# Two-layer conditional experts on one core: where the routing groups, one activation and the last layer-0 pair's products stand in the order of work

## The chip, the cores and the metric

The kernel runs on one core of a Trainium2 chip. A core has five engines that run side by side, each with its own queue of instructions: TensorE (matmul), VectorE, ScalarE, GpSimd (called POOL in the profile) and SyncE (SP), which issues most DMA transfers. The metric is the device time of one execution in microseconds (us), less is better.

## The reference

Each of 16 samples has 256 positions of width 256, all in 32 bits. Layer 0 gives each sample one of 8 experts; layer 1 gives it a weighted sum of two experts and adds a shared expert.

```python
# layer 0: one expert for each sample
expert = jnp.argmax(opcode_onehot, axis=-1)
up   = einsum('bsd,bhd->bsh', x, W_up[expert])   + b_up[expert]      # 512 wide
gate = einsum('bsd,bhd->bsh', x, W_gate[expert]) + b_gate[expert]
x = x + einsum('bsh,bdh->bsd', silu(up) * gate, W_down[expert]) + b_down[expert]
# layer 1: two of 8 experts and the shared one, 1024 wide
rw = softmax(cond)
w, sel = top_k(rw, 2)
w = w / w.sum(-1)
w = w / 12 + (1 - 1 / 12) * stop_gradient(w)
mlp = lambda g, u, d: (gelu_tanh(x @ g) * (x @ u)) @ d
x = x + sum_k w_k * mlp(skill_gate[sel_k], skill_up[sel_k], skill_down[sel_k]) \
      + mlp(shared_gate, shared_up, shared_down)
```

## The kernel before

**Routing.** The samples are sorted on VectorE by their expert, so that two samples with the same expert can be worked on as a pair; the shared expert's pairs need no routing. For layer 1 the sort is recorded as a list of groups of VectorE instructions (`steps`, filled through `Recorder` and `step`). `route` (L1013) issues the next group; all its instructions have line 1017 in the profile. Most groups are one operation over 128x1024 numbers. `routes` (L1007) says how many groups are issued at the start of a quarter.

**A pair of samples.** A pair is computed with a 2x2 block scheme of seven products instead of eight (`STEPS`): A blocks are weights (`q`, and their sums `s`, made on POOL by `sums_a`, L524 to L527), B blocks are activations (and their sums, made on VectorE by `sums_b`, L517 to L519). The up projections are cut along the hidden dimension: 2 quarters in layer 0 and 4 in layer 1, each with seven steps up0 to up6 (L586) of two matmuls, or four records. Quarters are counted by `line.at`: 0 and 1 are the first single sample of layer 0, 2 and 3 the second, 4 to 11 the four layer-0 pairs (two quarters each), and 12 to 15 the first pair of samples in the shared expert, which is layer 1. For the data of this run a further layer-0 pair follows as 16 and 17, then the shared expert's next pair.

**Banks and readers.** Products accumulate in PSUM banks X, Y and Q, two of each; A and B, one each, serve the down products together with Y. up0, up1, up3 and up5 open a bank; up2 and up4 go on with the X of up0, and up6 with the Q of up3. ScalarE copies X out after up0, up2 and up4 (`copy`, L567). VectorE combines the copies with Y or Q into the four blocks of `c` (`combine`, L571): C11 after up1, C22 after up4, C21 after up5, C12 after up6. A bank can be opened again, or gone on with, once its readers are through. Then comes the activation (`act`: silu with a bias on ScalarE in layer 0, L616; gelu in layer 1, L622), the product of the two halves (L628, VectorE) and `act_sums` of it. The seven down steps (L660) are read by `early` (L677 on VectorE, or L682 on ScalarE) and `late` (L693 and L689 on VectorE).

**The order.** Everything is issued in an order that a small planner, `Line`, gives. It has a clock: each of up0 to up5 issues, adds 2, and then issues all that has come due. So a quarter is 12 long. `later(n, f)` makes f due n after now; of two things due together, the one put down first comes first. For quarter j, which begins at T and ends at T+12, up6 is due 4 after its end, the second half of a layer-0 activation 3, the activation and product 6, and the sums of the product 12. With `crowded` set, the product comes 9 after the end, behind C22 of the next quarter, and a layer-0 pair's sums of down weights 14 instead of 12 after the start of its second quarter. A pair's down steps follow its last quarter at `first`, `first + step` and so on. At the start of a quarter, `ahead` prepares later ones: the weights five quarters on, the `q` sums three on, and the sums of the next pair's x (`sums_x`) 5 after the quarter's start. The engines' queues are in order, so this order is also the order in which a waiting instruction holds up those behind it. Between quarters 11 and 12 the program branches on the number of further layer-0 pairs (`tc.Switch`).

Of the kernel before, what the change touches and what calls it, by code (L numbers as in the profile page):

```python
# [55 lines left out]
UP, SINGLE_UP = 2, 8  # L56
# [3 lines left out]
def kernel(  # L60
# [71 lines left out]
    def when_free(tag, f):  # L132

        if turns[tag] and not turns["later", tag]:
            f()
        else:
            turns["later", tag].append(f)
# [361 lines left out]

    class Pair(Unit):  # L500
        width, last = 2, False
        crowded = False
        first, step = 18, None

# [218 lines left out]
        def run(self, line, among):  # L723

            self.start()
            for j in range(self.kp):
                line.quarter(self, j)
                for k in range(6):
                    line.main(UP, lambda j=j, k=k: self.up(j, k))

                line.later(2 * UP, lambda j=j: self.up(j, 6))
                if not self.layer:
                    line.later(UP + 1, lambda j=j: self.act0(j, 1))
                if self.last and j == self.kp - 1:

                    line.later(1, lambda: self.act_half(j, 0))
                    line.later(2 * UP, lambda: self.act_half(j, 1))
                else:
                    self.ended[j] = line.clock
                    line.later(3 * UP, lambda j=j: when_free("bt", lambda: self.act(j)))  # L740
                line.later(6 * UP, lambda j=j: self.act_sums(j))
                for f in among[j] if j < len(among) else ():
                    f()
            step = self.step or (6 if self.layer else 3)
            for k in range(7):
                line.later(self.first + step * k, lambda k=k: self.down(k))
# [113 lines left out]
    l0_pairs = [Pair(next(names), 0, 2 * i) for i in range(NP1)]  # L860
# [3 lines left out]
    shared = [Pair(next(names), 1, None, (2 * i, 2 * i + 1)) for i in range(NPR)]  # L864
    pairs = [Pair(next(names), 1, 2 * i) for i in range(NP2)]
    more_pairs = [Pair(next(names), 1, 2 * NP2 + 2 * i) for i in range(MOST[1])]
    ones = [Single(next(names), 1, 2 * NP2 + i) for i in range(NS2)]
    for u in l0_pairs[:-1]:
        u.crowded = True
        u.first = 16.5  # L870
    shared[-1].last = True
    shared[-2].step = 7
# [42 lines left out]
    class Line:  # L915
# [64 lines left out]
        def quarter(self, unit, j):  # L980

            self.at += 1
            assert quarters[self.at] == (unit, j)
            self.ahead(self.at)
            self.send()
            for layer in range(2):
                for i, (*at, engines) in enumerate(announces[layer]):
                    if [unit, j] == at:
                        self.announce(layer, engines, i == 0)
            for _ in range(self.routes(unit, j)):  # L990
                self.route()

        def announce(self, layer, engines, first):

# [11 lines left out]

        def routes(self, unit, j):  # L1007

            if not unit.layer:
                return {2: 5, 3: 1}.get(self.at, 0)  # L1010
            return int(j < 3) + (unit is shared[0] and j == 0)

        def route(self):  # L1013

# [12 lines left out]
    line = Line()  # L1027
# [54 lines left out]
    def follow(units, behind=True):  # L1082
# [3 lines left out]
        if known == start + Q_AHEAD - 1:  # L1086
            u, j = quarters[known]
            u.load_q(j, behind=behind)

    run(units[0])  # L1090
    for k in arms(0):

# [10 lines left out]
        for a, p in zip(places[4:], pieces):  # L1103
            a.append(p)
        follow([*mid, *units[1], *tails[1]], behind=False)
        run([*mid, *units[1]])
        while line.routed < len(steps):
            line.route()
        for k in arms(1):
            left = ones[2 * k :]  # L1110
            rest = [*tails[1], *left[:-1], *more_pairs[:k], *shared[1 - NB :]]
            turns["xs"], turns["d"] = [0, 1], [*turns["d"], 2]
            for u in rest:
                among[u] = [[] for _ in range(u.kp)]
            if left:

                host = rest[len(left)]
                for j in range(host.kp):
                    among[host][j].append(partial(left[-1].piece, line, j, among=True))
                left[-1].po_bank, left[0].po_bank = "A", "B"  # L1120
                shared[-NB].first = 24
            follow(rest)
            run(rest)
            line.flush(1 << 30)
            line.send()
# [58 lines left out]
```

## Time and profile before

| What | Value |
| --- | --- |
| Time, median of 3 runs | 1047.77 us (1046.82 to 1048.23) |
| Profiled execution, whole time | 1047.03 us |
| Profiled execution, span | 1045.4 us |
| Granted TensorE clock, mean | 0.998 |
| TensorE, VectorE, ScalarE, POOL busy | 1035.3, 755.1, 371.0, 444.0 us |
| Matmuls | 4746 |
| HBM traffic | 150 GB/s over the span |

The span runs from the first to the last instruction of one profiled execution; the whole time has a little around it. A busy share is an average over the whole span. The views that answer for one place are the waits (who waited for whom, and how long), the timeline of one engine (start, duration, and in brackets the idle time before an instruction and what ended it), and the table by windows (busy time of each engine and the granted clock in a stretch). In the tables, `Y<-xt,q` means that tile Y was written from tiles xt and q.

### The profile page before, as it was taken

The page shows a single profiled execution, that of the slowest core. Times are in us where ns is not written, and L with a number is a line of the kernel's source. Part 1 is how long each engine was busy: PE and PEld are TensorE (multiplying, and loading weights), DVE is VectorE, ACT ScalarE, POOL GpSimd, SP SyncE. Part 2 cuts the span into 40 slices and gives each one's busy share as a digit, 9 for nine tenths or more (in the row PEclk, how much of TensorE's full clock was granted, in tenths as well). Part 3 has the DMA queues.
Part 4 walks back from the last instruction along what each step waited for, and adds up shares of the span by engine and source line. Part 5 has one row for each costly group of instructions (what it writes and reads, how often), then busy time and mean ns, then how long its engine had stood idle before and what let it go on. Part 6 is the DMA issues. An engine that isn't in the chain of part 4 may idle for free.

```text
span 1045.4 us, 14150 instructions
## 1 busy us (share of the span) xinstructions
PE 1035.3 (99%) x4746; PEld 900.7 (86%) x4746; DVE 755.1 (72%) x1213; ACT 371.0 (35%) x584; POOL 444.0 (42%) x509
## 2 busy tenths in 40 slices
PE   9999999999999999999999999999999999999998
PEld 7887888888888888888888888888888888888887
DVE  8799978878687767777777777777765235777764
ACT  2444353535333333333333333333333123333331
POOL 3865231221034665566467556755201255620000
PEclk9999999999999999999999999999999999999999
DMA  7654756657664355245425533542655445366532
GB/s 266 220 182 146 249 171 197 206 164 239 202 229 125 89 141 142 98 104 141 108 82 134 141 104 98 141 133 72 179 164 170 131 136 156 91 181 181 185 78 45
DMA packets 61118, 157.47 MB, mean 151 GB/s; under 512 B 7522, under 2 KB 27362, under 8 KB 56802
## 3 DMA queue, kind: packets, MB, share of 16 engines
q1 hardware_dynamic: 47762, 140.90, 39.8%
q0 software_dynamic: 12976, 15.21, 10.1%
q8 instruction: 42, 0.69, 0.3%
q14 instruction: 50, 0.41, 0.1%
q10 hardware_dynamic: 288, 0.26, 0.1%
HBM read 132.23 MB, written 24.12 MB: 150 GB/s over the span
## 4 chain that ended last, share of the span: by engine, by line
PE 94%; DVE 4%; issue 1%; ACT 0%; DMA 0%; SPq 0%; DVEq 0%; ACTq 0%
PE X L586 25%; PE Q L586 17%; PE Y L586 17%; PE A L660 13%; PE B L660 9%; PE Y L660 9%; PE X L758 2%; PE Q L758 1%; PE A L788 1%; DVE c L571 1%; PE B L788 1%; DVE bt L628 1%; PE Y L788 0%; DMA lg<-cond_dram 0%; DVE bt L517 0%
## 5 line engine op out<-in xcount | busy, mean ns | idle before, releaser
L567 ACT ACTIVATE cp<-X 128x512 f32<-128x512 f32 x318 | 189.5, 596 | 508.3 <-PE X L586 507.9
L628 DVE TENSOR_TENSOR bt<-c 128x1024 f32<-128x1024 f32 x105 | 144.8, 1379 | 121.9 <-ACT c L622 114.4
L586 PE MATMUL Y<-xt,q 128*128 128x256 f32 x736 | 189.5, 380 | 2.0 <-DVE c L571 1.7
L586 PE MATMUL Q<-xt,s 128*128 128x256 f32 x736 | 189.5, 380 | 0.4 <-DVE c L571 0.4
L586 PE MATMUL X<-xt,s 128*128 128x256 f32 x736 | 189.5, 380 | 0.0
L571 DVE TENSOR_TENSOR c<-cp,Q 128x512 f32<-128x512 f32 x212 | 144.4, 681 | 41.8 <-ACT cp L567 37.2
L571 DVE TENSOR_TENSOR c<-cp,Y 128x512 f32<-128x512 f32 x212 | 144.2, 680 | 22.9 <-PE Y L586 22.1
L586 PEld LDWEIGHTS Y<-xt,q 128*128 128x128 f32 x736 | 139.8, 190 | 22.4 <-DVE c L571 2.3
L586 PEld LDWEIGHTS Q<-xt,s 128*128 128x128 f32 x736 | 139.3, 190 | 21.0 <-DVE c L571 2.3
L586 PEld LDWEIGHTS X<-xt,s 128*128 128x128 f32 x736 | 139.3, 190 | 20.5 <-ACT cp L567 1.4
L487 POOL DMA_DIRECT2D out_dram<-ys x46 | 49.1, 1075 | 207.4 <-DVE ys L689 128.6
L524 POOL TENSOR_TENSOR s<-q 128x256 f32<-128x256 f32 x78 | 66.3, 849 | 150.0 <-PE Q L586 86.9
L527 POOL TENSOR_TENSOR s<-s,q 128x256 f32<-128x256 f32 x78 | 63.4, 813 | 128.8 <-PE Q L586 128.8
L660 PE MATMUL B<-bt,ds 128*128 128x256 f32 x420 | 101.3, 381 | 0.7 <-DVE ys L693 0.7
L660 PE MATMUL A<-bt,ds 128*128 128x256 f32 x420 | 100.5, 379 | 0.0
L622 ACT ACTIVATE c<-c 128x1024 f32<-128x1024 f32 x91 | 95.6, 1051 | 6.5 <-DVE c L571 6.3
L586 PE MATMUL X<-xt,q 128*128 128x256 f32 x368 | 95.3, 382 | 0.0
L660 PEld LDWEIGHTS B<-bt,ds 128*128 128x128 f32 x420 | 79.9, 191 | 12.2 <-issue 1.0
L660 PE MATMUL Y<-bt,d 128*128 128x256 f32 x376 | 90.0, 379 | 0.0
L660 PEld LDWEIGHTS A<-bt,ds 128*128 128x128 f32 x420 | 79.7, 190 | 11.2 <-issue 0.3
L517 DVE TENSOR_TENSOR bt<-bt 128x512 f32<-128x512 f32 x112 | 86.8, 775 | 0.1
L525 POOL TENSOR_TENSOR s<-s,q 128x256 f32<-128x256 f32 x78 | 78.1, 1002 | 6.1
(179 smaller groups left out, 1141.1 us busy)
## 6 DMA issues: line engine op xcount, KB each, us to landing
q<-wq_dram SPq DMA_DIRECT2D x114, 512.0 KB, 3.7
d<-wd_dram SPq DMA_DIRECT2D x22, 1024.0 KB, 6.4
s<-qsums SPq DMA_DIRECT2D x28, 512.0 KB, 4.9
xt<-x1d SPq DMA_DIRECT2D x46, 256.0 KB, 3.9
out_dram<-ys POOLq DMA_DIRECT2D x46, 256.0 KB, 4.5
ds<-dsums SPq DMA_DIRECT2D x7, 1024.0 KB, 6.2
d<-wd_dram SPq DMA_DIRECT2D x7, 513.0 KB, 5.6
bt<-x_dram SPq DMA_DIRECT2D x14, 256.0 KB, 4.7
```

The lines of the kernel that those rows point to most:

```text
L487: store = nc.gpsimd.dma_start(row(out), ys[:, :, t, :], accum_op=ALU.add)
L517: tt(t[:, 4:6, :], t[:, 0:3:2, :], t[:, 2:4, :], ALU.subtract)
L524: tt(s("S1"), a("A21"), a("A22"), ALU.add)
L525: tt(s("S2"), s("S1"), a("A11"), ALU.subtract)
L527: tt(s("nS4"), s("S2"), a("A12"), ALU.subtract)
L567: nc.scalar.activation(t, self.banks["X", j], AF.Copy)
L571: nc.vector.tensor_tensor(self.c[j][:, block].rearrange("p m s -> p (m s)"), self.copies[n, j], self.banks[tag, j], op,)
L586: nc.tensor.matmul(self.banks[tag, j][:, bass.ts(m, S)], lhsT=self.q[j][:, m, A_AT[a], :] if a in A_AT else self.s[j][:, m, S_AT[a], :], r ...
L622: nc.scalar.activation(u, u, AF.Gelu_apprx_tanh)
L628: nc.vector.tensor_tensor(t[:, 0:4, :], u, v, ALU.mult)
L660: nc.tensor.matmul(d, lhsT=src[:, j, :], rhs=self.acts[j][:, B_AT[b], :], start=OPENS[k] and j == 0, stop=j == self.kp - 1, skip_group_che ...
L758: nc.tensor.matmul(dst[:, bass.ts(half, S)], lhsT=self.q[j][:, m, 2 * half + c, :], rhs=self.xt[:, c, :], start=(c == 0), stop=(c == KD - 1),)
```

## The change

Three things in the order of work are changed; no instruction's operands are.

- Routing groups: in a pair's quarter a group is issued 5 after the start, behind what was due then (a `sums_x` put down before it), up6 of the quarter before and up2, and no longer at the start. The two groups of quarter 12 are issued in quarters 5 and 6, one each. Quarters 13 and 14, and the later ones, keep one group each.
- The activation of the first layer-0 pair's second quarter (number 5) is due 9 after its end and no longer 6, so behind the copy and C22 after up4 of quarter 6.
- The last layer-0 pair (quarters 10 and 11) is `crowded` like the others: its products come 9 after the quarter's end, and its sums of down weights 14 instead of 12 after the start of quarter 11. Its `first` stays at 18.

```diff
     class Pair(Unit):
         width, last = 2, False
+        behind = None
         crowded = False
...
                     self.ended[j] = line.clock
-                    line.later(3 * UP, lambda j=j: when_free("bt", lambda: self.act(j)))
+                    act = lambda j=j: when_free("bt", lambda: self.act(j))
+                    line.later(9 if j == self.behind else 3 * UP, act)
                 line.later(6 * UP, lambda j=j: self.act_sums(j))
...
+    for u in l0_pairs:
+        u.crowded = True
+
+    l0_pairs[0].behind = 1
     for u in l0_pairs[:-1]:
-        u.crowded = True
         u.first = 16.5
...
             for _ in range(self.routes(unit, j)):
-                self.route()
+
+                self.later(5 if unit.width == 2 else 0, self.route)
+            self.flush(self.clock)
...
         def routes(self, unit, j):
             if not unit.layer:
-                return {2: 5, 3: 1}.get(self.at, 0)
-            return int(j < 3) + (unit is shared[0] and j == 0)
+                return {2: 5, 3: 1, 5: 1, 6: 1}.get(self.at, 0)
+            return int(j < 3 and (unit is not shared[0] or j > 0))
```

## The prediction

> **What bounds the kernel.** The page first: which engine is full.
>
> ```profile
> PE 1035.3 (99%) x4746; PEld 900.7 (86%) x4746; DVE 755.1 (72%) x1213; ACT 371.0 (35%) x584; POOL 444.0 (42%) x509
> ```
>
> TensorE has no share left to win but its own gaps. In its timeline an undisturbed step (four records of 128x256) follows the one before after 0.8635 us, so 4,740 such matmuls want 1,023.2 us; from the first (6.00) to the end of the last (1,040.86) the trace has 1,034.9. About 11.7 us are lost in all: that is the ceiling of any re-ordering. Next, TensorE's waits, to see where:
>
> ```profile
> PE Y L586 <- DVE c L571: 1.7, 1, 1.7
> PE B L660 <- DVE ys L693: 0.7, 1, 0.7
> PE Q L586 <- issue: 0.5, 1, 0.5
> ```
>
> The first two are neighbours. TensorE's timeline there (start, us, engine, line, tiles; the idle before a group and its releaser in brackets):
>
> ```profile
> 91.81 1.03 PE L586 MATMUL X<-xt,q 128*128 128x256 f32 x4
> 92.68 1.03 PE L660 MATMUL B<-bt,ds 128*128 128x256 f32 x4
> 93.93 1.13 PE L586 MATMUL Y<-xt,q 128*128 128x256 f32 x4 [0.23 <-DVE ys L693]
> ...
> 101.94 1.13 PE L586 MATMUL Y<-xt,q 128*128 128x256 f32 x4 [1.70 <-DVE c L571]
> 103.75 1.73 PE L660 MATMUL B<-bt,ds 128*128 128x256 f32 x4 [0.68 <-DVE ys L693]
> 105.28 1.91 PE L586 MATMUL X<-xt,q 128*128 128x256 f32 x4
> 106.99 1.28 PE L586 MATMUL Y<-xt,q 128*128 128x256 f32 x4
> ...
> 108.96 1.03 PE L586 MATMUL X<-xt,s 128*128 128x256 f32 x4
> ```
>
> This is quarter 12, the shared expert's first, and the start of 13. From 91.81 to 108.96 there are 14 steps, worth 12.09 us; they took 17.15, so 5.06 us are lost in one place. The steps at 103.75 to 106.99 are twice as long as they should be though nothing holds them. The answer by windows says why (the third number from the end is the granted clock):
>
> ```profile
> 104.00:108.00 4.00, 4.00 (x12) 3.17 (x12) 3.97 (x7) 0.93 (x2) 0.00 (x0) 0.57 0.86 301
> ```
>
> What held TensorE is in VectorE's timeline:
>
> ```profile
> 91.80 1.74 DVE L628 TENSOR_TENSOR bt<-c 128x1024 f32<-128x1024 f32 x1
> 93.47 0.41 DVE L693 TENSOR_TENSOR ys<-dz,Y 128x256 f32<-128x256 f32 x1
> ...
> 98.15 0.61 DVE L1017 TENSOR_TENSOR wts<-wts,den 128x16 f32<-128x16 f32 x2
> ...
> 99.54 1.75 DVE L1017 TENSOR_TENSOR ys<-num 128x1024 f32<-128x1024 f32 x1
> 101.21 0.68 DVE L571 TENSOR_TENSOR c<-cp,Y 128x512 f32<-128x512 f32 x1
> ```
>
> The product at 91.80 (L628, quarter 10) stands ahead of the L693 that frees bank Y: the 0.23. Two routing groups (L1017) fill 98.15 to 101.21, 3.06 us, ahead of the combine C11 of quarter 12, which frees the Y bank that step up5 opens: the 1.70. The late L693 for B stands three instructions behind: the 0.68.
>
> The "issue" wait is in quarter 7's start, in VectorE's and ScalarE's timelines:
>
> ```profile
> 44.73 0.67 DVE L571 TENSOR_TENSOR c<-cp,Q 128x512 f32<-128x512 f32 x1
> 47.29 0.69 DVE L571 TENSOR_TENSOR c<-cp,Q 128x512 f32<-128x512 f32 x1 [1.88 <-ACT cp L567]
> ```
> ```profile
> 45.44 1.33 ACT L616 ACTIVATE c<-c,bq 128x512 f32<-128x512 f32 x2 [1.72 <-DVE c L571]
> 46.68 1.06 ACT L567 ACTIVATE cp<-X 128x512 f32<-128x512 f32 x2
> ```
>
> up6 of quarter 6 accumulates into bank Q after C22 has read it (47.29 to 47.98). C22 waited for the copy of X, and that stood behind the activation of quarter 5, which itself waited for VectorE. Between 46.53 and 49.02, two steps took 2.49 us: 0.76 lost.
>
> **The change, part by part.**
>
> *Two groups leave quarter 12.* 3.06 us of VectorE ahead of C11 go. With part 3, and every VectorE time in this stretch taken at its slow value (1.74 for the product, 0.94/0.83/0.83 for the sums: the rows beside a busy POOL), the order after is: sums of quarter 12's x end 91.88; L693 91.80 to 92.21 (TensorE wants that Y at 93.54: no wait); C22 of 11 to 92.8; product of 10 to 94.4; C21 95.0; early L677 95.4; sums of 10 to 98.05; C11 of 12 to 98.7. TensorE at its pitch wants that bank for up5 at 99.59: 0.9 to spare. C12, two L677, then L693 for B, done 100.4; the B step is due at 100.45, so 0 to 0.2 lost. Both idles go, hence the clock loss behind them.
>
> Here one rule is weighed. The trace: idles of 1.70 and 0.68 us, then a granted mean of 0.57 over 104 to 108, where the three steps from 103.75 to 108.10 took 4.35 us instead of 2.59. The span's mean of 0.998 leaves room for about 2 us so lost: this place and no other. The Trainium skill, "TensorE: Matmul & The Clock Gate", section "Why this matters for your kernels", says the clock drops when TensorE idles more than about 3 us between bursts. By it these idles were too short, the halving is no part of this stall and could stay: only 5.06 less 1.76, or 3.3, would come back. By the trace, where the halving follows the only large idle and comes nowhere else, all 5.06. I take the trace, and 0.1 off for B: **4.95**.
>
> *Where they go.* The group of four small ones (98.15 to 99.54: 1.39 us) goes into quarter 5 behind C12 of quarter 4 (ends 36.5), where VectorE then idles 2.81 us until 39.34: nothing. If that cover were gone it would cost up to 1.4. The 128x1024 comparison goes into quarter 6 behind the 44.73 row, into the 1.88 idle. It costs 1.22 (its sister z<-ats at 108.41) to 1.75 (beside POOL), so it ends 46.55 to 47.1.
>
> *Activation behind a copy.* ScalarE's copy for C22 no longer waits for 45.44: X is done 44.97, so copy 45.0 to 45.6, activation to 46.9 (its product, issued behind C22 before and after, is not late). C22 now starts when the comparison ends, 46.6 to 47.1, instead of 47.29; up6 is due 47.39 and needs C22's end plus 0.1. Saved: 0.15 to 0.76 of the 0.76; I take **0.4**. VectorE is not idle from 47.29 to 64.21, so the 0.49 us TensorE loses between 55.92 and 60.73 moves with it and stays.
>
> *Last layer-0 pair.* The product of 10 goes behind L693 and C22 (counted). That of 11 goes behind C22 of 12: its activation waits for C12 (99.3), runs 1.33, the copy follows at 100.6 to 101.2, C22 to 101.9 (up6 due 103.04), product to 103.1. It is needed first by the down product A at 104.77: 1.7 to spare, 0. POOL's down sums of this pair (84.94 to 88.5) fall behind the next quarter's q sums and its qsums store: those can run before 87, so down sums to 91.2, or 98 if the q sums stay at 89.88. First use was at 114.14, 109 now: at least 11 us of cover. No SP transfer changes its place in SP's queue.
>
> *Later groups, each from a quarter's start to behind C12.* Behind C12 VectorE mostly waits for ScalarE's gelu (the page: 121.9 us before L628, 114.4 of it for L622), about 1.1 us, what a group takes: nothing, and C11 and C12 come earlier. Where no such idle is, a price: the long group at 172.27 to 174.91 now pushes the next product to 178.3 and the L693 that frees Y to 180.5, which is when TensorE wants it: 0 to 0.3, I take 0.1. At 303 TensorE loses 0.69 behind a chain in which two routing bits (0.18) precede C11: they leave it, **0.15** back. The 0.32 lost at 115.66 hangs on C12, the table load and gelu: stays, 0 to 0.6.
>
> Sum: 4.95 + 0.4 + 0.15 - 0.1 = **5.4 us**. The profiled execution (1,045.4 span, 1,047.03 in all) becomes 1,041.6; it lies 0.74 under the median, within the runs' 1.4, so between the two bases, 1,041.6 and 1,042.4: **1,042.0**.
>
> **The rivals.**
> 1. *The clock stays lost* (10%): a remaining idle, B's or another, still costs one such window. Gain 5.4 less 1.7: 1,043.7; with a half of the idle left, 1,044.5. For it: the rule above. Against: the record.
> 2. *The stall moves to the last pair's down products* (5%, no change): product of 11 now waits for activation, copy and C22 in a row. It costs nothing until it ends after 104.77; 3 us beyond that, with a new 1.7 us clock loss, give back 4.7: about 1,047. Against it: 1.7 us of slack with slow values.
> 3. *VectorE has no room early* (5%, slower): if the stretch from 44.73 to 98 is one backlog, work put in at quarters 5 and 6 comes out at quarter 12 all the same; the 5.06 stay, and 1.75 more at up6 of quarter 6 with a clock loss of 1.7 gives 1,051. It decides if the idle before 47.29 is not really freed by the copy. For it: layer 0's stretch 50 to 92 has VectorE busy 40.38 of 42. Against: it waits for ScalarE's copies at 64.21 (0.26) and 82.34 (0.78), so no backlog lives that long.
>
> **How the numbers follow.** My forecast has 80%. Its least: 5.06 less 0.2 for B and 0.3 for the later groups, with 0.15 at quarter 7: 4.7, from the median 1,043.1; its most, with all of 0.76, 0.49, 0.69 and 0.32 back, 7.3: 1,040.1 midway between the bases. The range takes rival 1 in: 1,040.4 to 1,044.6. 0.2% (2.1 us) is what a measurement can tell from no change; forecast and rival 1 pass it: 0.90 faster; rival 2 mostly same, 0.04; rival 3 and the rest slower, 0.06.
>
> **What would show it.** PEclk full from 92 to 110; TensorE's 14 steps there in about 12.2 us; no L1017 between 90 and 100; L1017 in VectorE's idles near 36 and 45; the copy ahead of L616 near 45; L693 ahead of the 1.74 product. Wrong if the wait on c L571 stands elsewhere, above all before A near 105, or if up6 near 47 waits longer than now.

## The result, and the profile after

The changed kernel takes 1,041.32 us (median of 6 runs, 1,040.21 to 1,044.96) against 1,048.0 for the kernel before (6 runs): ratio 0.9943, 95% interval 0.9925 to 0.9962, or 6.7 us less. A second series of the same kernel gave 1,041.48 (5 runs, 1,041.14 to 1,041.77), ratio 0.9942 (0.9929 to 0.9956). The profiled execution of the first series took 1,044.96, with a span of 1,043.2; it is one of two of the eleven runs that stand at 1,044 or above. The forecast was 1,042.0. "First profile" and "second profile" below are the profiled executions of these two series (1,044.96 and 1,041.48).

Line numbers are shifted in the changed kernel: L572 is the combine, L629 the product, L678 `early`, L694 `late`, L1025 a routing group. First TensorE's timeline in quarter 12 and what follows (start, us, engine, line, tiles):

```profile
91.82 1.03 PE L587 MATMUL X<-xt,q 128*128 128x256 f32 x4
...
99.59 1.03 PE L587 MATMUL Y<-xt,q 128*128 128x256 f32 x4
100.45 1.03 PE L661 MATMUL B<-bt,ds 128*128 128x256 f32 x4
...
103.91 1.03 PE L587 MATMUL X<-xt,s 128*128 128x256 f32 x4
...
108.22 1.03 PE L587 MATMUL Y<-xt,q 128*128 128x256 f32 x4
110.63 1.10 PE L661 MATMUL A<-bt,ds 128*128 128x256 f32 x4 [1.38 <-DVE dz L678]
111.57 1.03 PE L587 MATMUL X<-xt,q 128*128 128x256 f32 x4
113.28 1.13 PE L587 MATMUL Y<-xt,q 128*128 128x256 f32 x4 [0.68 <-DVE ys L694]
```

The fourteen steps from 91.82 to 103.91 take 12.09 us, which is exactly their undisturbed time: all 5.06 us are back, and the windows of 4 us from 92 to 112 all have a granted clock of 1.00. But two idles are new, at 109 and 112. VectorE's timeline shows both sides of it:

```profile
97.72 0.69 DVE L572 TENSOR_TENSOR c<-cp,Y 128x512 f32<-128x512 f32 x1 [0.16 <-issue]
...
99.71 0.41 DVE L694 TENSOR_TENSOR ys<-dz,B 128x256 f32<-128x256 f32 x1
...
104.27 0.96 DVE L519 TENSOR_TENSOR bt<-bt 128x256 f32<-128x256 f32 x1
105.26 1.38 DVE L520 TENSOR_TENSOR bt<-bt 128x256 f32<-128x256 f32 x1
...
107.76 2.33 DVE L1025 TENSOR_TENSOR z<-ats 128x1024 f32<-128x1024 f32 x1
110.01 0.47 DVE L678 SCALAR_TENSOR_TENSOR dz<-A,d,bt 128x256 f32<-128x256 f32 x1
```

C11 of quarter 12 ends at 98.4 and the B reader at 100.1, 1.2 and 0.3 us before TensorE wants them. Two things then delay VectorE. Two sums ahead of quarter 13's C11 take 0.96 and 1.38 us, and quarter 13's routing group behind C12 takes 2.33; L678 behind the group frees bank A 1.4 us late. In the second profile of the same kernel the same four instructions are 2.2 us shorter in sum:

```profile
103.48 0.42 DVE L519 TENSOR_TENSOR bt<-bt 128x256 f32<-128x256 f32 x1
103.94 0.83 DVE L520 TENSOR_TENSOR bt<-bt 128x256 f32<-128x256 f32 x1
...
105.89 1.21 DVE L1025 TENSOR_TENSOR z<-ats 128x1024 f32<-128x1024 f32 x1
107.02 0.47 DVE L678 SCALAR_TENSOR_TENSOR dz<-A,d,bt 128x256 f32<-128x256 f32 x1
```

L678 is through at 107.5, and TensorE takes the step on A at 108.56, so there is 1.1 us to spare. TensorE's waits have neither idle:

```profile
PE Y L160 <- DVE cp L157: 1.6, 1, 1.6
PE Q L587 <- DVE c L572: 0.4, 1, 0.4
PE A L661 <- DVE dz L678: 0.4, 1, 0.4
```

That is the usual run; the 1.6 is at the start, the 0.4 on Q at 298 and the 0.4 on A at 59. ScalarE's timeline of the first profile shows the order that the second part of the change makes, the copy ahead of the activation:

```profile
45.76 0.60 ACT L568 ACTIVATE cp<-X 128x512 f32<-128x512 f32 x1 [1.34 <-PE X L587]
46.25 1.32 ACT L617 ACTIVATE c<-c,bq 128x512 f32<-128x512 f32 x2
```

In that profile the order gained nothing yet: TensorE had lost 0.6 us at up4 of quarter 6 (44.56), the group in quarter 6 ended at 47.39, and C22 and up6 came when they had come before the change (up6 at 48.09 against 48.08). In the second profile the group ends earlier, and C22 and up6 follow 0.7 and 0.6 us earlier:

```profile
45.39 1.24 DVE L1025 TENSOR_TENSOR ys<-num 128x1024 f32<-128x1024 f32 x1
46.55 0.67 DVE L572 TENSOR_TENSOR c<-cp,Q 128x512 f32<-128x512 f32 x1
```
```profile
47.45 1.03 PE L587 MATMUL Q<-bt,s 128*128 128x256 f32 x4
```

One thing about the kernel before is seen only in the list of its runs. One stretch of half clock during the work costs 1.7 of the 1,045 us and so takes the mean granted clock of an execution to 0.998 or less; all profiled executions without such a stretch have 0.999 or 1.000. Of the 70 further runs of the kernel before that were made beside the experiments, 23 have 0.998 or less (median 1,048.16) and 47 have 0.999 or more (median 1,047.56). By this count the profile that the forecast was reckoned from, with its half clock, shows the rarer case, and the usual run is only 0.6 us faster than such a run, not 1.7. What it loses instead is not known: none was profiled.

### The profile page after: what moved, and what is told of

Same layout as the page of the kernel before. It is cut to its first block, busy times and chain, and to the rows that moved or that the text cites. A ratio compares the mean times of both kernels' runs of the same rounds, so it can differ in the third digit from the quotient of the medians.

```text
span 1043.2 us, 14149 instructions
## 1 busy us (share of the span) xinstructions
PE 1033.6 (99%) x4746; PEld 900.5 (86%) x4746; DVE 760.9 (73%) x1213; ACT 371.0 (36%) x584; POOL 444.9 (43%) x509
## 4 chain that ended last, share of the span: by engine, by line
PE 88%; DVE 1%; issue 0%; ACT 0%
PE X L587 23%; PE Q L587 16%; PE Y L587 16%; PE A L661 12%; PE B L661 8%; PE Y L661 8%; PE Q L760 1%; PE X L760 1%; PE B L790 1%; PE A L790 1%; DVE bt L629 0%; DVE c L572 0%; ACT c L623 0%; DVE xt L520 0%; DVE ys L694 0%
## 5 line engine op out<-in xcount | busy, mean ns | idle before, releaser
L629 DVE TENSOR_TENSOR bt<-c 128x1024 f32<-128x1024 f32 x105 | 146.4, 1394 | 114.9 <-ACT c L623 111.8
L572 DVE TENSOR_TENSOR c<-cp,Q 128x512 f32<-128x512 f32 x212 | 144.3, 681 | 40.8 <-ACT cp L568 33.3
L572 DVE TENSOR_TENSOR c<-cp,Y 128x512 f32<-128x512 f32 x212 | 144.1, 680 | 27.1 <-PE Y L587 25.9
```

The lines of the kernel that those rows point to most:

```text
L572: nc.vector.tensor_tensor(self.c[j][:, block].rearrange("p m s -> p (m s)"), self.copies[n, j], self.banks[tag, j], op,)
L629: nc.vector.tensor_tensor(t[:, 0:4, :], u, v, ALU.mult)
```

## The experiments

Ratios are to the kernel before, run on the same chip with each set (its medians 1,047.4 to 1,048.0), with 95% intervals. The last four rows are the set whose kernel before has 1,047.4, half a microsecond less than the others, so a difference between medians of different sets is good to about half a microsecond.

| Kernel | Median us (runs) | Ratio |
| --- | --- | --- |
| changed, first series | 1,041.32 (6) | 0.9943 [0.9925, 0.9962] |
| changed, second series | 1,041.48 (5) | 0.9942 [0.9929, 0.9956] |
| no group in 13, one more in 16 | 1,041.57 (5) | 0.9948 [0.9935, 0.9962] |
| all groups at the start | 1,045.27 (15) | 0.9977 [0.9969, 0.9985] |
| routing part alone | 1,042.32 (5) | 0.9952 [0.9938, 0.9965] |
| group of 13 twice | 1,043.94 (5) | 0.9965 [0.9951, 0.9978] |
| without the activation part | 1,042.37 (5) | 0.9952 [0.9938, 0.9966] |
| last-pair part alone | 1,046.26 (21) | 0.9988 [0.9982, 0.9995] |
| activation part alone | 1,046.79 (21) | 0.9992 [0.9985, 0.9999] |
| group of 13 at the start | 1,043.93 (6) | 0.9967 [0.9955, 0.9979] |
| groups of 5, 6 at the start | 1,042.85 (5) | 0.9961 [0.9948, 0.9975] |
| both in 5 | 1,041.24 (5) | 0.9943 [0.9930, 0.9957] |
| both in 5, none in 13, one in 16 | 1,041.66 (5) | 0.9945 [0.9932, 0.9959] |

**The changed kernel again.**

> The changed kernel once more, for a second profile: the first profiled execution took 1044.96 us while four of its six runs took 1040.2 to 1041.4. Theory A (the new idles of 1.38 and 0.68 us near 109 to 113, behind quarter 13's routing group that took 2.33 us beside POOL's down sums, are not in every execution): a profile of a run near 1041 shows the group in about 1.2 us and less idle there. Theory B (the spread is elsewhere: start of the clock, the tail): the same idles of about 2 us stand near 109 to 113 and the runs differ by the time at which the full clock begins. Median 1041 to 1042.5 by both.

Theory A: the run is 3.5 us faster than the profiled one of the first series, and between 104 and 120 us TensorE loses 0.1 us instead of 2.6. The second profile's full clock began at 6.8 us instead of 7.6, which accounts for about 0.4 of the rest. The theory named the group alone; the rows above show the two sums ahead of it as the other half of the delay.

**Is it the group of quarter 13?** Issued twice:

```diff
-                for f in steps[self.routed]:
+                for f in steps[self.routed] * (2 if self.at == 13 else 1):
                     f()
```

> The changed kernel with quarter 13's one routing operation issued twice in a row (about 1.2 us more of VectorE at that place, in every execution; the result of the operation is the same). Theory A (the slower profile of 1044.96 us is that group taking 2.33 us instead of 1.21, with the L678 for A behind it): idles of about 1.4 us before A and 0.7 us before Y come back in the profile and the time is 2 to 3.5 us above the changed kernel's: 1043.5 to 1045. Rival (the group has about a microsecond to spare there, and the slow profile had another cause): within 0.7 us of 1041.4.

1,043.94, as forecast, and its waits are nearly those of the first profile; below them the two copies of the group on VectorE:

```profile
PE A L661 <- DVE dz L678: 1.5, 2, 1.3
PE Y L587 <- DVE ys L694: 0.7, 1, 0.7
```
```profile
106.04 3.43 DVE L1025 TENSOR_TENSOR z<-ats 128x1024 f32<-128x1024 f32 x2
```

The two copies take 3.43 us, 2.2 more than the 1.21 of one in the second profile (not 1.2, as was meant). So 2.2 us more of VectorE at that one place, as much as the first profile has, costs 2.5 us and makes these two idles, and the rival is out. It does not show that one slow group is enough: with 1.1 us to spare, a group of 2.3 just fits, and in the profile of the routing part alone (below; a group is L1022 there) it does:

```profile
104.97 2.23 DVE L1022 TENSOR_TENSOR z<-ats 128x1024 f32<-128x1024 f32 x1
```

TensorE does not wait behind that one. Taking the group away from quarter 13:

```diff
-                return {2: 5, 3: 1, 5: 1, 6: 1}.get(self.at, 0)
-            return int(j < 3 and (unit is not shared[0] or j > 0))
+                return {2: 5, 3: 1, 5: 1, 6: 1, 16: 1}.get(self.at, 0)
+            return int(j < 3 and (unit is not shared[0] or j > 1)) + (self.at == 16)
```

> The changed kernel, with quarter 13's routing group left out there and issued in quarter 16 instead. Theory A (that group, slowed by POOL's sums, holds the L678 and the product behind it): the idles near 109 to 113 (2.25 us more lost than before the change) go, no new one at quarter 16 where VectorE waits about 1.1 us for gelu; 2 us less than the changed kernel: 1039 to 1040. Rival (the backlog there comes from the last pair's later products, and the next instruction in line waits as long): idles of 1 us or more stay at the same place, 1041.

The groups are issued in a fixed order, so this moves quarter 13's group into quarter 14 (at 114.05) and quarter 14's into 16. 1,041.57: no gain over the usual run, which has no idle there to win, and none of its five runs is above 1,043; five runs are too few to tell whether the two slow ones of eleven are gone. My 1,039 to 1,040 was reckoned from the first profile, and missed.

**Where the routing groups stand within a quarter.** All of them back at the quarter's start, with the new counts:

```diff
-                self.later(5 if unit.width == 2 else 0, self.route)
+                self.later(0, self.route)
```

> The changed kernel, but groups of pairs are issued at the quarter's start again (the counts by quarter are the new ones: one in 5, one in 6, none in 12). My reading: nearly all the gain is in where the two groups go, not in their place within a quarter: quarter 5 and 6 at the start stand ahead of C11, so C22 of 5 and 6 come later by what VectorE does not idle, at most 1 us lost near 48; near 108 the group stands ahead of C11 and C12, the gelu comes 1.2 to 2.3 us later and the idle there is as long or longer. Expected 1041 to 1043. Rival (placing them behind C12 is what brings the time): 1044 or more.

1,045.27: the rival. More than half of the gain is lost again, 3.8 us. Its profile has one large wait, 1.96 us for the L694 that frees Y in quarter 14. So the group of quarter 13 was put back alone, and then the two early ones alone:

```diff
-                self.later(5 if unit.width == 2 else 0, self.route)
+                self.later(5 if unit.width == 2 and self.at != 13 else 0, self.route)
```

> The changed kernel with quarter 13's group alone back at the quarter's start; all others stay behind C12. Theory (the 3.9 us between the changed kernel and the one with all groups at the start come from this one group, because it delays C12, hence the gelu, the product and the L694 for Y that quarter 14 waits for): an idle of about 2 us before that Y and a half clock behind it, 1044.5 to 1046. Rival (the loss is spread over the later quarters): less than 1 us above the changed kernel.

```diff
-                self.later(5 if unit.width == 2 else 0, self.route)
+                self.later(5 if unit.width == 2 and self.at not in (5, 6) else 0, self.route)
```

> The changed kernel with the groups of quarters 5 and 6 at the quarter's start; all others stay behind C12. Theory as for the quarter 13 group: little is lost here. In quarter 5 VectorE idles afterwards; in quarter 6 C11 and C12 come 1.2 us later and C22 as before, the activation of quarter 5 (which waits for C12) 1.2 us later: 0 to 0.7 us above the changed kernel, 1041.4 to 1042.1. Rival: 1044 or more.

Quarter 13 alone costs 2.5 us (1,043.93, a little under the 1,044.5 to 1,046 I gave; its profiled execution, 1,045.12, lay within). VectorE's timeline in that execution:

```profile
104.53 2.29 DVE L1025 TENSOR_TENSOR z<-ats 128x1024 f32<-128x1024 f32 x1
106.74 0.67 DVE L572 TENSOR_TENSOR c<-cp,Y 128x512 f32<-128x512 f32 x1
107.33 0.68 DVE L572 TENSOR_TENSOR c<-cp,Q 128x512 f32<-128x512 f32 x1
107.93 0.47 DVE L678 SCALAR_TENSOR_TENSOR dz<-A,d,bt 128x256 f32<-128x256 f32 x1
109.13 2.36 DVE L629 TENSOR_TENSOR bt<-c 128x1024 f32<-128x1024 f32 x1 [0.73 <-ACT c L623]
111.41 0.68 DVE L572 TENSOR_TENSOR c<-cp,Q 128x512 f32<-128x512 f32 x1
112.01 0.41 DVE L694 TENSOR_TENSOR ys<-dz,Y 128x256 f32<-128x256 f32 x1
```

Ahead of C11 the group delays C12 (107.33), on which gelu waits, then product, C22 and the L694 for Y, and TensorE waits 1.96 us. Behind that the clock is halved (two windows; the first figures are length and TensorE's busy time, the third from the end is the granted clock):

```profile
109.33:112.75 3.42, 1.46 (x7) 0.98 (x6) 3.42 (x4) 0.85 (x2) 1.64 (x2) 1.00 0.75 274
112.75:116.16 3.41, 3.41 (x9) 2.71 (x9) 2.71 (x6) 0.00 (x0) 0.00 (x0) 0.50 0.47 192
```

That is the slowest of its six runs; two of the six lost the clock by their mean (0.998 or less), as did 4 of the 15 with all groups at the start and none of the changed kernel's eleven. Behind C12 the group lies where VectorE would wait for gelu anyway: in the run with no group in 13 the product waits 1.13 us for it. The groups of 5 and 6 cost 1.4 us at the start (1,042.85), twice the most that I had allowed; TensorE then loses 1.0 us between 46 and 55, where the changed kernel's second profile has nothing, and about as much as that one near 57 to 60. The two make 3.9 against 3.8 for all together, but with half a microsecond open in each, so that a share of the later quarters is neither shown nor excluded; it was not tried. Nor was the simplest alternative, both groups left in quarter 12 but put behind its C12.

**Each part alone.** The routing part alone is the changed kernel without `behind` and with the last pair as before; the other two are the kernel before with that part's lines.

> The kernel before with the routing part alone (groups moved and put behind C12; no change to the activation or to the last pair). By my sums the routing part carries the gain of quarter 12 but for the 0.4 us that the product at 91.80 costs there, and loses the 0.4 us of the copy near 48, where the group in quarter 6 makes nothing worse: 1042 to 1043. If the last pair's part is what makes the new idle near 109, that idle is gone here and the time is 1040 to 1041. If the parts need each other (rival), the idle near 100 stays in part with its clock loss: 1044 or more.

> The kernel before with the third part alone (the last layer-0 pair's products behind C22). My sums: the L694 for Y no longer stands behind the product at 91.80, 0.4 us back, but both groups are still in quarter 12, so the idle of 1.7 us and the lost clock stay: 1047.2 to 1048. Rival (the product is what delays C11 there, since VectorE's work ahead of it is the same): the idle at up5 shrinks by more than 1 us and the clock stays full, 1045 or less.

> The kernel before with the second part alone. With no group in quarter 6 the copy lets C22 start at about 45.6 instead of 47.29: up6's 0.76 us are gone, and VectorE is 1.6 us earlier from there on, so that the 0.49 us lost between 56 and 61 go too. The idle in quarter 12 stays, or shrinks by nothing, since VectorE waits for copies twice before it. 1046.5 to 1047.2. Rival (VectorE's backlog lasts to quarter 12): 1.6 us of it go there too, the clock stays full, 1043 to 1044.

The routing part alone gives 1,042.32, within its forecast and 5.6 us of the whole gain: no idle from 61 to 120, though the last pair's products are where they were. The last-pair part alone gives 1.8 us, not 0.4, and fits neither of my two cases: the idle at up5 shrinks and the clock stays full, as the rival said, but the time does not follow, because the wait comes back later. Its TensorE waits:

```profile
PE Y L586 <- DVE c L571: 1.1, 1, 1.1
PE Y L586 <- DVE ys L693: 0.8, 1, 0.8
PE B L660 <- DVE ys L693: 0.7, 1, 0.7
```

The 1.1 is not up5 of quarter 12 any more but of quarter 13 (at 111.09), ahead of which stands a group of 2.29 us; at quarter 12 the two groups took 1.8 us (97.67 to 99.51) instead of 3.06 and left 0.13. No half clock follows in this execution (by the mean clock, in one of 21 runs), and its span is 1.2 us shorter. The activation part alone gives 1.2 us, the number that was forecast, but by another way: in its profile (execution of 1,046.99) the idle at up5 of quarter 12 is 0.7 and no longer 1.7, B's is 0.7 as before, and the large idle, 2.0 with the half clock behind it, now stands in quarter 14. So in the kernel before, time given back early is in part lost again at a later place.

> The changed kernel without its second part (the activation of quarter 5 stands ahead of the copies again). From the two profiles: up6 of quarter 6 waits again, 0.76 us, of which some 0.3 comes back where VectorE is late near 58: 1041.9, 0.4 us slower than the changed kernel. If the idle before C22 there (0.72 us with the group in place) is not what holds up6: no difference.

Without the activation part 1,042.37: it is worth about 0.9 us here, not 0.4; between 34 and 63 us TensorE loses 2.0 in this profile and 1.2 in the changed kernel's second. up6 of quarter 6 waits 0.52 us again in that profile:

```profile
PE Q L587 <- POOL s L527: 0.5, 1, 0.5
```

(the releaser named is POOL, which had long been done; C22 is what up6 follows). This kernel has the last pair's part and equals the routing part alone (1,042.32), so on top of the routing the last pair's part brings nothing that these runs can tell.

**A better place for the two groups?**

```diff
-                return {2: 5, 3: 1, 5: 1, 6: 1}.get(self.at, 0)
+                return {2: 5, 3: 1, 5: 2}.get(self.at, 0)
```

> The changed kernel with both moved groups in quarter 5 and none in quarter 6. VectorE idles 1.27 us there after the first group; the second takes 1.21 to 1.75: it fits, or delays C22 of 5 by up to 0.5. C22 of quarter 6 then starts near 45.6 instead of 46.55, VectorE is 1 us earlier from there, and the 0.6 us lost between 56 and 60 go: 1040.6 to 1041. If POOL's sums hold the second group up, C22 of 5, and the copy behind the activation of 5, come late: no gain, 1041.5 to 1042.

> The same with quarter 13's group in quarter 16 as well, so that no group stands near POOL's down sums at 104 to 112. By the sum of the two: 1040.6 to 1041 and no run above 1043. If the group's move to 16 costs its own time there (as the run with that move alone, 1041.57, allows): 1041 to 1041.5.

1,041.24 and 1,041.66: neither beats the changed kernel. With both in quarter 5 the loss near 58 does vanish in the profile, and TensorE waits for the copy that up4 of quarter 6 needs, which stands behind the activation that waits for C21 of 5:

```profile
PE X L587 <- ACT cp L568: 0.5, 1, 0.5
```

That this place causes the wait is not shown. The same wait (0.4 to 0.5) stands in the changed kernel's first profile and in those with the group of 13 at the start and with the activation part alone, where no second group is in quarter 5. All four have the product ahead of that C21 at 1.7 to 1.8 us, beside POOL, and the second profile, without the wait, has it at 1.33.

## Why the prediction was right, point by point

- *The 5.06 us of quarter 12*: right, step by step, for the profiled execution. C11 of 12 ended at 98.4 (98.7 in the working), the reader of B at 100.1 (100.4), the product of 11 at 102.7 (103.1). The 0.1 off for B was not needed.
- *The clock*: all of it came back, as the trace said; the other reading that the prediction weighed would have left 1.76. Three experiments lost it again in their profiles, each behind about 2 us of idle. But it was taken for a loss of every run, and by the mean clock 47 of 70 runs of the kernel before do not have it. Their median, 1,047.56, is still 6.1 above the changed kernel's, so those runs lose nearly as much in some other place. The prediction did not look for that, and this part of its agreement is luck.
- *The two groups in quarters 5 and 6*: right, and for the reason given: in the second profile the second one takes 45.39 to 46.63, C22 follows at 46.55 and up6 is not held.
- *The activation behind the copy*: right in kind, too small. 0.4 was taken; in the second profile the whole 0.76 came back at up6 (in the first one nothing, see above), and the pair of runs says 0.9 in all.
- *The last pair*: in the sum, the 0.39 at bank Y was put down to it. The routing part alone has no wait there either: with POOL elsewhere in time, the product takes 1.22 us and not 1.74. On top of the routing it brings nothing that the runs can tell, though 1.8 us alone; a gain that two edits share was counted once, rightly, but booked to one of them.
- *Groups behind C12*: booked at nothing, and here the reasoning was too short. Without this step 3.8 us of the gain are lost again: with TensorE on time, the group of quarter 13 at the start is the next 2 us wait, in some runs with the half clock behind it. The profile before did not show it, because TensorE arrived there 5 us late. What saved the sum is that the change moved this group too; the prediction gives another reason for the move.
- *Quarter 13*: "0 to 0.6" was given for Y, and nothing for A; no time was reckoned for L678, which now stands behind the group. It has 1.1 us to spare in the second profile and is 1.4 us late in the first, with slow sums and a slow group. Where that happens TensorE loses 2.57 us between 104 and 120 (0.12 in the second profile). By the times it was in 2 of 11 runs; only one of these two was profiled.
- *303*: 0.15 was booked, and none came: TensorE loses 0.70 there in both profiles, as before. Nor was there a price at 180.
- *Rivals*: of the three, the second named a stall moved to the last pair's down steps. That is where it went in the first profile, through the reader of A and not through the product of 11. The first (the clock stays lost) and the third (no room early) did not come.

Profile for profile the sum was nearly exact: 1,041.6 was reckoned from the execution of 1,047.03, and the second profile's took 1,041.48. By the medians the gain is 6.4 to 6.7 and not 5.4. The activation (0.5 more), the price at 180 and B (0.1 each) and 303 (0.15 less) make about 0.5 of that difference; the rest is not assigned and lies within the intervals. That 1,042.0 comes so close is in part chance: it starts from 1,047.4, and the kernel before has 1,048.0 in this series.

## What to carry to other kernels

When a wait is removed, walk on along the engine that caused it with the waiting engine on time: the next instruction of the same kind may have been harmless only because everything arrived late. Work that is not urgent belongs behind the instruction on which another engine's chain depends (here C12 and gelu), in the wait that follows it anyway, and not at the start of a stage. And read two executions before a gain is judged, of the kernel before too: one profile here was 3.5 us from the usual run, and the only one of the kernel before has a half clock that two thirds of its runs do not have.

## What the runs showed of the hardware

**The clock.** The trace's record of the granted clock puts each half-clock stretch at 3.41 us, and its start at a whole number of such stretches after the first full clock: in the kernel before 5.08 to 104.07 us is 29.0 times 3.413. In these profiles the stretch just before it decides. TensorE was busy for 1.45 or 1.46 us of it in all four profiles in which the clock was halved during the work (the kernel before, all groups at the start, the group of 13 at the start, the activation part alone), and for 2.07 and 2.12 in the changed kernel's first profile and with the group twice, in which it was not:

```profile
100.66:104.07 3.41, 1.45 (x6) 1.00 (x7) 3.12 (x7) 1.55 (x3) 1.21 (x1) 1.00 0.00 0
104.07:107.48 3.41, 3.41 (x10) 2.66 (x9) 3.41 (x6) 0.52 (x2) 0.00 (x0) 0.50 0.87 300
```
```profile
109.97:113.38 3.41, 2.07 (x9) 1.54 (x9) 3.41 (x6) 0.60 (x1) 1.82 (x2) 1.00 0.84 277
```

The first pair is the kernel before, the last row the changed kernel's first profile. So the idles of 1.70 and 0.68 us in the kernel before were enough; whether an idle of some 2 us costs the clock depends on how it falls into these stretches.

The end of the program narrows the limit down. There TensorE runs out of work, and the record halves the clock in all fourteen profiles, but not always after the last stretch with work. In the kernel before, that stretch has 1.54 us of TensorE, and the next one still has the full clock:

```profile
1039.32:1042.73 3.41, 1.54 (x8) 1.00 (x6) 0.69 (x2) 0.00 (x0) 0.00 (x0) 1.00 0.44 125
1042.73:1046.15 3.42, 0.00 (x0) 0.00 (x0) 0.00 (x0) 0.00 (x0) 0.00 (x0) 1.00 0.07 19
```

With the group twice it is 1.61 us, and the same; with no group in 13 and one more in 16 it is 1.33, and the next stretch has half the clock. So in these profiles the limit lies between 1.46 and 1.54 us of TensorE's busy time, as the trace counts it, in a stretch of 3.41.

**VectorE beside POOL.** When one of these VectorE operations over two tiles in SBUF and a POOL operation overlap in these traces, the one that starts second takes about its own duration and what is left of the other's. In the changed kernel's first profile POOL starts 0.03 us ahead of the group at 107.76, and the group takes 2.33; in the second the group (105.89) starts 0.09 us ahead, takes 1.21, and POOL is the one that takes long:

```profile
107.73 1.27 POOL L527 TENSOR_TENSOR ds<-d 128x512 f32<-128x512 f32 x1
```
```profile
105.98 2.24 POOL L526 TENSOR_TENSOR ds<-ds,d 128x512 f32<-128x512 f32 x1
```

Less than a tenth of a microsecond decides which engine waits. By itself this group's wait is not what TensorE's 2.5 us hang on: the group of 2.23 us in the routing part alone costs nothing. In the first profile the two sums ahead of it had lost 1.1 us in the same way, beside the POOL operations at 104.22 and 104.91. This is read from the rows; no run varied the overlap by itself.
